# A graph layer and a mixture of experts on one core: up products of the ranked lists as seven block products

## The chip, the cores and the metric

The kernel runs on one NeuronCore of a Trainium2 chip. The metric is the device time of one execution in microseconds (us); less is better. The program has five engines that matter here: TensorE (PE in the profile, its weight loads PEld), VectorE (DVE), ScalarE (ACT), GpSimd (POOL) and SyncE (SP), which issues most transfers. Each engine works through its own instructions in a fixed order.

## The reference

There are 3327 tokens of 256 features. A graph attention layer over a 3327 x 3327 adjacency comes first, then a mixture of 16 experts of which each token uses its two best:

```python
x = x + _L0_gnn_ref(_layernorm(x), adj, W, a, gamma, beta)
...
xn = _layernorm(x)                                  # 256 features
logits = xn @ gate_w + gate_b                       # 16 experts
top_probs, top_idx = jax.lax.top_k(softmax(logits), 2)
top_probs = top_probs / sum(top_probs)
h1 = xn @ w1[e]                                     # 256 -> 512
h2 = xn @ w2[e]                                     # 256 -> 512
expert_out = (silu(h1) * h2) @ w3[e]                # 512 -> 256
x = x + sum over the two experts of top_probs * expert_out
```

All products of the experts are in float32. The two matrices w1 and w2 make the "up" products, w3 the "down" product.

## The kernel before

The graph part works first, in seven groups of up to four tiles of 128 tokens. As groups are finished, their tokens are gated, their normalised rows are stored to a buffer in HBM, and tables are made that say which token belongs to which expert. The experts' part then works through 19 lists of tokens (`take_list`, L1031). Lists 0 to 2 and 3 to 5 hold the tokens of experts 0 to 2, from the early and the late groups; lists 6 to 18 are the other 13 experts, ranked by the number of their tokens and called ranked lists here. A list has a fixed width, `ROOM` (L87): for lists 6 to 18 it is 512, 512, 480, 472, 416, 408, 400, 400, 392, 392, 376, 376 and 336 columns. Tokens beyond the room would be done in a loop behind (L1216), which these inputs do not enter.

One list goes as follows. GpSimd gathers the list's rows from HBM (`gather`, L960, one indirect DMA for each tile of 128 rows, into one of three buffers `XE`). VectorE works out the weights of the rows (`weigh`, L964). The rows are transposed to `xt`, with features on partitions: for lists below 8 on TensorE through the two PSUM banks "pt" (L1060, copied out by ScalarE at L1071), from list 8 on in `by_halves` (L1004) by DMA transposes of 16-bit halves, with copies in front (L1025 on ScalarE, L1026 on VectorE) and behind (L1028 on ScalarE, L1029 on VectorE). The copies behind write `xt`, of which there are two.

Then come the up products (`up_products`, L974). The 256 input features are KC = 2 blocks of 128, the 512 hidden features JC = 4 blocks of 128. For each hidden block j and each of w1 and w2, two matmuls of 128 x 128 weights against all n columns of the list add up over the input blocks in one of four PSUM banks "pa" (L976). Each program matmul is two instructions in the profile, since the operands are float32. ScalarE makes the gate `s` by Silu out of one bank (L1081), VectorE multiplies it with the other bank into `hid` (L1084). So a list has 16 program matmuls of n columns for its up products.

The down products (`down_products`, L978) take 128 tokens at a time: four matmuls with `hid` as weights and w3 of 256 columns as the moving side, in one of two banks "ph" (L987); for a last tile of up to 64 tokens, column tiles of the array share the work (L983). VectorE scales the rows by their token weights (L1102, and L1104 for the parts of a short tile); for lists 0 to 2 ScalarE does it for full tiles (L1100, `helped`). GpSimd adds the rows to the output by an indirect DMA with addition (`add_rows`, L989).

The order of all of this is not written out by hand. Every piece of work is registered with `plan.add`, with an engine, an estimated duration, a rank, the works that it follows and the buffers that it uses (`Plan`, L114). The planner places at each step the work that can start earliest, the lower rank first among equals (L171). A buffer kind has a number of slots (`SLOTS`, L372), and a further user waits for the oldest slot's users to end. Between engines it reckons 0.2 us (`HOP`). It draws 80 orders, replays them with disturbed durations and keeps the best (L203). The order then stands in the program; on the chip an engine waits at each instruction for what it needs. For a list i the rank on TensorE is (4, i, 0) for the transposes, (4, i, 1 + j) for the up products and (4, i, 9 + t) for the down products.

The weights of an expert are loaded by SP (`load_weights`, L325) into one of four sets of tiles, `w1e`, `w2e` and `w3e` (L332); the loads of list i are released by the gathers of list i - 2 (L1201).

Of the kernel before, what the change touches and what calls it, by code (L numbers as in the profile page):

```python
# [47 lines left out]
F32 = mybir.dt.float32  # L48
# [6 lines left out]
P = 128  # L55
# [3 lines left out]
D = 256  # L59
# [21 lines left out]
TURNED = 2 * EARLY + 2  # L81

# [134 lines left out]
def gnn_moe(ctx: ExitStack, tc: tile.TileContext, x, adj_t, W, a, gamma, beta, gate_w, gate_b, w1, w2, w3, out):  # L217
# [114 lines left out]
    def weight_tiles():  # L332
        return [POOLS["wmore"].tile([P, k, n], F32, name=name)
                for name, k, n in (("w1e", KC, HID), ("w2e", KC, HID), ("w3e", JC, D))]
# [33 lines left out]
    def few_h(key):  # L368
# [5 lines left out]
             "turned": 2}  # L374
# [19 lines left out]
        "turned": lambda key: POOLS["turns"].tile([P, 2 * KC, CAP], U16, name="turned_rows"),  # L394
        "y": lambda key: POOLS["gates"].tile([P, D], F32, name="y", bufs=SLOTS["y"]),
# [15 lines left out]
    def psum(key):  # L411
        return T[key]
# [565 lines left out]
    def down_products(py, w3e, hid, t, m):  # L978
        if PARTS[m] > 1:

            for j in range(JC):
                c = j % PARTS[m] * (P // PARTS[m])
                nc.tensor.matmul(py[c:c + m, :D], hid[:, j, t * P:t * P + m], w3e[:, j, :], start=(j < PARTS[m]),  # L983
                                 stop=(j >= JC - PARTS[m]), tile_position=(0, c))
            return
        for j in range(JC):
            nc.tensor.matmul(py[:m, :D], hid[:, j, t * P:t * P + m], w3e[:, j, :], start=(j == 0), stop=(j == JC - 1))  # L987
# [43 lines left out]
    def take_list(i, indexed, stored, weights, opened, order):  # L1031
# [14 lines left out]
        def w_of(k):  # L1046
            return WE[weights][k]
# [26 lines left out]
        for j in range(JC):  # L1074
# [3 lines left out]
                for b, key in enumerate(keys)]  # L1078

# [9 lines left out]
        for t, mm in tiles:  # L1089
            key, yk = ("ph", "list", i, t), ("y", i, t)  # L1090
            w = plan.add(PE, 8 * 0.217 / PARTS[mm] + 0.1 * (PARTS[mm] > 1), rank + (9 + t,), hids, lambda t=t, mm=mm, key=key: down_products(
                psum(key), w_of(2), hid(), t, mm), [key, hk] + ([wk] if weights else []))


            helped = i < EARLY and PARTS[mm] == 1
# [79 lines left out]
    def switch_pools():  # L1175
        gnn.close()
        POOLS["wmore"] = ffn.enter_context(tc.tile_pool(name="wmore", bufs=4))
        POOLS["hidden"] = ffn.enter_context(tc.tile_pool(name="hidden", bufs=2))
        POOLS["turns"] = ffn.enter_context(tc.tile_pool(name="turns", bufs=2))
        POOLS["gates"] = ffn.enter_context(tc.tile_pool(name="gates", bufs=3))  # L1180
# [24 lines left out]
    order, told = [], []  # L1205
# [82 lines left out]
```

## Time and profile before

| | us |
|---|---|
| median of 3 runs | 524.83 |
| lowest and highest run | 521.37, 528.43 |
| profiled execution, its time | 525.92 |
| profiled execution, its span | 524.0 |
| first up product of list 6, from the span's start | 285.06 |
| first down product of list 18, from the span's start | 512.63 |
| DVE, ACT, POOL busy over the span | 287.9, 173.1, 216.3 |

The span runs from the first to the last instruction in the trace; the execution's time has 1.9 us more around it. A line of the trace's timeline names the start and the length in us, the engine, the line of the kernel, the operation, output and inputs, the shape (partitions x elements), and how many instructions were merged; in brackets stand the idle time of the engine ahead of it and what ended that. A line of the waits names who waited for whom, the us in total, the times and the longest. PE's lengths overlap, since matmuls are pipelined; PEld is the load of weights, which runs beside the matmuls. TensorE ran at its full clock nearly throughout (a mean of 0.995).

### The profile page before, as it was taken

Reading aid. Unit: us, or ns where it says so; the run is one execution under the profiler, and the core shown is the slowest. Engines: PE = TensorE matmul, PEld = TensorE weight load, DVE = VectorE, ACT = ScalarE, POOL = GpSimd, SP = SyncE. Lnnn points to the kernel's source line nnn. Section 1 sums busy time; section 2 is a strip of 40 time slices with the busy share of each in tenths; the row PEclk is TensorE's granted clock in tenths of the full one; section 3 lists DMA queues with packets and bytes.
Section 4 is the critical chain, followed back from the end, with each engine's and each line's share of the span. In section 5 each row is a group of like instructions: output and inputs, shape, how many; then the busy total and the mean of one; then the engine's idle time right before and its main releaser. Section 6 shows DMA issues by size and latency. Waiting matters only on the chain. (4 is left out here: it accounts for less than half of the span.)

```text
span 524.0 us, 8563 instructions
## 1 busy us (share of the span) xinstructions
PE 508.0 (97%) x2923; PEld 400.0 (76%) x2924; DVE 287.9 (55%) x870; ACT 173.1 (33%) x464; POOL 216.3 (41%) x240
## 2 busy tenths in 40 slices
PE   9999999999999999999999979999999999999995
PEld 6789999999999999876778454665766566666773
DVE  5878564886969799768932234233333544334221
ACT  2462153635372741474222134132222212121110
POOL 4230022121031411737676667665644644224333
PEclk9999999999999999999999989999999999999999
DMA  8932889797879896454479778857867875542222
GB/s 274 357 134 79 306 254 306 244 321 248 264 218 366 284 350 205 147 184 115 83 236 346 145 167 171 179 122 191 155 130 186 200 180 99 130 138 30 29 31 28
DMA packets 85698, 100.01 MB, mean 191 GB/s; under 512 B 27150, under 2 KB 59154, under 8 KB 85652
## 3 DMA queue, kind: packets, MB, share of 16 engines
q1 hardware_dynamic: 74612, 85.42, 52.7%
q0 software_dynamic: 10768, 13.75, 15.9%
q8 instruction: 24, 0.39, 0.3%
q10 hardware_dynamic: 272, 0.26, 0.1%
q14 instruction: 22, 0.18, 0.1%
HBM read 81.55 MB, written 13.75 MB: 182 GB/s over the span
## 5 line engine op out<-in xcount | busy, mean ns | idle before, releaser
L589 PE MATMUL pa<-hi,mk 128*128 128x258 f32 x676 | 167.6, 289 | 0.0
L590 PE MATMUL pa<-lo,mk 128*128 128x256 f32 x676 | 163.2, 281 | 0.0
L990 POOL DMA_INDIRECT out<-y,out_index x61 | 96.4, 1580 | 110.0 <-DVE y L1102 92.7
L589 PEld LDWEIGHTS pa<-hi,mk 128*128 128x128 f32 x676 | 127.7, 189 | 1.1 <-issue 1.0
L590 PEld LDWEIGHTS pa<-lo,mk 128*128 128x128 f32 x676 | 127.5, 189 | 0.1
L976 PE MATMUL pa<-xt,w2e 128*128 128x512 f32 (+12 forms) x272 | 97.7, 482 | 0.0
L976 PE MATMUL pa<-xt,w1e 128*128 128x512 f32 (+12 forms) x272 | 97.1, 479 | 0.0
L987 PE MATMUL ph<-w3e,hid 128*128 128x256 f32 (+5 forms) x400 | 91.3, 384 | 4.2 <-DVE hid L1084 3.4
L987 PEld LDWEIGHTS ph<-w3e,hid 128*128 128x128 f32 (+5 forms) x400 | 75.2, 190 | 19.2 <-DVE hid L1084 3.8
L1081 ACT ACTIVATE s<-pa 128x512 f32<-128x512 f32 (+14 forms) x76 | 35.2, 464 | 135.9 <-PE pa L976 131.9
L976 PEld LDWEIGHTS pa<-xt,w1e 128*128 128x128 f32 x272 | 49.7, 190 | 35.8 <-issue 19.1
L976 PEld LDWEIGHTS pa<-xt,w2e 128*128 128x128 f32 x272 | 49.1, 190 | 36.2 <-issue 19.5
L961 POOL DMA_INDIRECT x<-normed,index x61 | 64.8, 1063 | 24.9 <-issue 19.2
L1084 DVE TENSOR_TENSOR hid<-s,pa 128x512 f32<-128x512 f32 (+14 forms) x76 | 39.3, 520 | 62.6 <-PE pa L976 53.3
L566 DVE TENSOR_SCALAR mk<-sg 128x2048 fp32r<-128x2048 f32 (+2 forms) x49 | 54.2, 1105 | 29.4 <-PE pa L590 28.3
L1102 DVE TENSOR_SCALAR y<-ph,weight 128x256 f32<-128x256 f32 (+10 forms) x54 | 25.9, 482 | 70.5 <-PE ph L987 63.3
L655 POOL TENSOR_TENSOR hp<-csum,c 128x512 f32<-128x512 f32 (+1 forms) x14 | 15.1, 1097 | 65.0 <-DVE c L651 65.0
L483 PE MATMUL ph<-w_sb,xnt 128*128 128x260 f32 x104 | 27.9, 405 | 1.0 <-DVE lo L489 1.0
L1025 ACT COPY halves<-x 128x1024 uint16<-128x1024 uint16 (+1 forms) x11 | 10.9, 987 | 52.5 <-DMA turned_rows<-halves 33.6
L483 PEld LDWEIGHTS ph<-w_sb,xnt 128*128 128x128 f32 x104 | 18.3, 195 | 5.2 <-DVE lo L489 1.4
L426 POOL TENSOR_SCALAR rs_x<-spread_x 128x4 f32<-128x4 f32 (+1 forms) x7 | 1.7, 241 | 48.3 <-ACT pay L432 45.2
L669 ACT ACTIVATE agg<-agg,c 128x64 f32<-128x64 f32 x76 | 18.8, 335 | 1.9 <-DVE c L651 1.8
(185 smaller groups left out, 485.2 us busy)
## 6 DMA issues: line engine op xcount, KB each, us to landing
sg<-in_adj_t SPq DMA_DIRECT2D x25, 1024.0 KB
sg<-in_adj_t SPq DMA_DIRECT2D x20, 768.0 KB
w1e<-in_ffn_w SPq DMA_DIRECT2D x15, 512.0 KB
w2e<-in_ffn_w SPq DMA_DIRECT2D x15, 512.0 KB
w3e<-in_ffn_w SPq DMA_DIRECT2D x15, 512.0 KB
normed<-pay SPq DMA_DIRECT2D x5, 520.0 KB
out<-x SPq DMA_DIRECT2D x5, 512.0 KB
sg<-in_adj_t SPq DMA_DIRECT2D x4, 576.0 KB
```

What stands on the lines that cost most here:

```text
L483: nc.tensor.matmul(ph[:, :H + D], T["xnt", g, t][:, k, :], w_sb[:, k, :], start=(k == 0), stop=(k == KC - 1))
L566: nc.vector.tensor_scalar(T[mk][:, :m, :n * P], T[sk][:, :m, :n * P], 0.0, None, op0=ALU.is_gt)
L589: nc.tensor.matmul(pa[:, :D + 2], lhs, HI[mg][:, i, H:], start=first, stop=False)
L590: nc.tensor.matmul(pa[:, :D], lhs, LO[mg][:, i, H:], start=False, stop=left[g, t] == 0)
L669: nc.scalar.mul(at, at, some("c")[:, 0, t, h:h + 1])
L961: nc.gpsimd.indirect_dma_start(out=xe[:, t, :], out_offset=None, in_=normed[:limit], in_offset=at_rows(idx, t), bounds_check=limit - 1, oo ...
L976: nc.tensor.matmul(p[:, :n], wt[:, k, j * P:(j + 1) * P], xt[:, k, :n], start=(k == 0), stop=(k == KC - 1))
L987: nc.tensor.matmul(py[:m, :D], hid[:, j, t * P:t * P + m], w3e[:, j, :], start=(j == 0), stop=(j == JC - 1))
L990: i = nc.gpsimd.indirect_dma_start(out=out, out_offset=at_rows(idx, t, m), in_=y[:m], in_offset=None, bounds_check=NP - 1, oob_is_err=Fals ...
L1081: nc.scalar.activation(T["gate", i, j][:, :n], psum(key)[:, :n], AF.Silu)
L1084: nc.vector.tensor_mul(hid()[:, j, :n], T["gate", i, j][:, :n], psum(key)[:, :n])
L1102: nc.vector.tensor_scalar(T[yk][:mm], psum(key)[:mm, :D], weight, None, op0=ALU.mult)
```

## The change

For lists 6 to 18 (`SEVEN` = 6) the up products are regrouped. Take a pair of hidden blocks (2 jp, 2 jp + 1), the two input blocks and the two halves of the list's columns. With weights a(c, k), c the hidden block of the pair and k the input block, and x blocks b(k, t), t the half of the columns, the four results are c(c, t) = a(c, 0) b(0, t) + a(c, 1) b(1, t), eight block products. Strassen's scheme (in Winograd's form) makes them with seven, out of sums of blocks:

- VectorE makes four sums of weight blocks for each list (one instruction each, 512 elements, for w1 and w2 and both pairs at once) and four sums of x blocks (half a list's width). Two of them overwrite a block in place; the others lie in slots of the older tiles "hp" and "agg" and in a new tile `xsum`.
- Each block product has one program matmul for w1 and one for w2, side by side in one bank (256 columns each).
- The products of a pair are p1, p5, p6, p2, p7, p3, p4 in this order. p1, p6 and p7 add up in one bank of "pt" (xx). ScalarE copies p1 from there to bank yy, where p2 is added; it copies p5 to SBUF (`qs`); after p6 VectorE writes the sum of xx and `qs` to bank zz, where p3 is added; after p7 ScalarE copies xx to bank vv, where p4 is added, and VectorE adds xx and `qs` to `c22`. So yy, zz, vv and `c22` are the four results.
- The four banks of "pa" become fixed banks for this (pq, py, pz, pv, one slot each). `fix_banks` opens them once by a bf16 matmul of 512 columns each, behind the last up products of list 5.
- Gates (ScalarE) and multiplies (VectorE) work on halves of the columns, eight of each for a list in place of four.
- The down products of these lists get the rank (4, i + 1, 9, t), that is behind the products of the next list, and a full tile's four matmuls are planned in two parts of two. The scaling of full tiles' rows goes to ScalarE.
- w1e and w2e become one tile.

The core of the diff:

```diff
-        return [POOLS["wmore"].tile([P, k, n], F32, name=name)
...
+        up = POOLS["wmore"].tile([P, 2, KC, HID], F32, name="w12e")
...
+             "turned": 2, "pq": 1, "py": 1, "pz": 1, "pv": 1, "qs": 2, "xsum": 2, "c22": 2}
...
+    FIXED = {}
+    CHAIN = []
+    def fix_banks():
+        for r in range(4):
+            FIXED[r] = psum(("pa", "fixed", r))
+            nc.tensor.matmul(FIXED[r], ones, ones[:, None, :].to_broadcast([P, CAP // P, P]), start=True, stop=True)
+    def by_sevenths(i, n, xts, loaded, fixed, xtk, wk, hk, weights):
+        half = n // 2
+        xsk, wsk, ask = ("xsum", i), ("hp", "list", i), ("agg", "list", i)
...
+        def combine(dst, one, other, op):
+            nc.vector.tensor_tensor(dst(), one(), other(), op=op)
+        def sums(cost, rank, after, uses, terms):
+            done, got = {}, []
+            for k, (name, dst, one, other, op, needs) in enumerate(terms):
+                done[name] = plan.add(DVE, cost, rank, after + [done[x] for x in needs],
+                                      lambda dst=dst, one=one, other=other, op=op: combine(dst, one, other, op), uses)
+            return done
+        S = sums(0.62, (2, i, 7), loaded, [wk, wsk, ask], [
+            ("1", lambda: ws(0), lambda: a(1, 0), lambda: a(1, 1), ALU.add, ""),
+            ("2", lambda: ws(1), lambda: ws(0), lambda: a(0, 0), ALU.subtract, "1"),
+            ("3", lambda: a(1, 0), lambda: a(0, 0), lambda: a(1, 0), ALU.subtract, "1"),
+            ("4", lambda: ws(2), lambda: a(0, 1), lambda: ws(1), ALU.subtract, "2")])
+        X_ = sums(0.1 + 0.55e-3 * n, (2, i, 6), xts, [xtk, xsk, ask], [
+            ("1", lambda: xs(0), lambda: b(0, 1), lambda: b(0, 0), ALU.subtract, ""),
+            ("2", lambda: xs(1), lambda: b(1, 1), lambda: xs(0), ALU.subtract, "1"),
+            ("3", lambda: b(0, 1), lambda: b(1, 1), lambda: b(0, 1), ALU.subtract, "1"),
+            ("4", lambda: xs(2), lambda: b(1, 0), lambda: xs(1), ALU.subtract, "2")])
+        base = xts + loaded
+        hids = []
+        def pair(jp):
+            xx, qq, yy, zz, vv, qs, cc = [(name, "seven", i, jp) for name in ("pt", "pq", "py", "pz", "pv", "qs", "c22")]
+            def product(number, after, key, lhs, rhs, first, more=()):
+                def emit(key=key, lhs=lhs, rhs=rhs, first=first, jp=jp):
+                    for w in range(2):
+                        nc.tensor.matmul(psum(key)[:, w * (CAP // 2):w * (CAP // 2) + half], lhs()[:, w, jp], rhs(),
+                                         start=first and w == 0, stop=True, skip_group_check=True)
+                return plan.add(PE, 4 * (0.44 * half / CAP + 0.003), (4, i, jp, number), after, emit, [key, xtk, xsk, wk, wsk, ask] + list(more))
+            def copy(src, key, at):
+                return plan.add(ACT, 0.14 + 0.9e-3 * n, (1, i, jp), [at], lambda: nc.scalar.copy(
+                    T[key][:, :, :half] if key == qs else both(psum(key)), both(psum(src))), [src, key])
+            def added(after, dst, more):
+                return plan.add(DVE, 0.16 + 1.02e-3 * n, (1, i, jp), after, lambda: nc.vector.tensor_tensor(
+                    dst(), both(psum(xx)), T[qs][:, :, :half], op=ALU.add), [xx, qs] + more)
+            p1 = product(0, base, xx, lambda: a(0, 0), lambda: b(0, 0), True)
+            p5 = product(1, [S["1"], X_["1"], p1, fixed], qq, lambda: ws(0), lambda: xs(0), True)
+            cy = copy(xx, yy, p1)
+            cq = copy(qq, qs, p5)
+            p6 = product(2, [cy, S["2"], X_["2"]], xx, lambda: ws(1), lambda: xs(1), False)
+            p2 = product(3, [cy], yy, lambda: a(0, 1), lambda: b(1, 0), False)
+            az = added([cq, p6], lambda zz=zz: both(psum(zz)), [zz])
+            p7 = product(4, [az, S["3"], X_["3"]], xx, lambda: a(1, 0), lambda: b(0, 1), False)
+            p3 = product(5, [az, S["4"]], zz, lambda: ws(2), lambda: b(1, 1), False)
+            cv = copy(xx, vv, p7)
+            ac = added([p7, cv, cq], lambda cc=cc: T[cc][:, :, :half], [cc])
+            p4 = product(6, [cv, X_["4"]], vv, lambda: a(1, 1), lambda: xs(2), False)
+            for j, t, made, key in ((0, 0, p2, yy), (0, 1, p3, zz), (1, 0, p4, vv), (1, 1, ac, cc)):
+                gk = ("gate", i, 2 * jp + j)
+                def part(w, key=key):
+                    return T[key][:, w, :half] if key[0] == "c22" else psum(key)[:, w * (CAP // 2):w * (CAP // 2) + half]
+                def gate(gk=gk, t=t, part=part):
+                    nc.scalar.activation(T[gk][:, t * half:(t + 1) * half], part(0), AF.Silu)
+                def multiply(gk=gk, j=j, t=t, jp=jp, part=part):
+                    nc.vector.tensor_mul(T[hk][:, 2 * jp + j, t * half:(t + 1) * half], T[gk][:, t * half:(t + 1) * half], part(1))
+                s = plan.add(ACT, 0.14 + 0.9e-3 * half, (1, i, jp, 9), [made], gate, [key, gk])
+                hids.append(plan.add(DVE, 0.16 + 1.02e-3 * half, (2, i), [s], multiply, [key, gk, hk]))
+        for jp in range(JC // 2):
+            pair(jp)
+        return hids
...
+        if i >= SEVEN:
+            if i == SEVEN:
+                CHAIN.append(plan.add(PE, 0.9, (4, i, -1), UPS, fix_banks, [("pa", "fixed", r) for r in range(4)]))
+            hids = by_sevenths(i, n, xts, opened, CHAIN[0], xtk, wk, hk, weights)
+        for j in range(JC if i < SEVEN else 0):
             keys = [("pa", "list", i, j, b) for b in range(2)]
             ups = [plan.add(PE, 4 * max(0.44 * n / CAP, 0.12), rank + (1 + j,), xts + opened, lambda j=j, b=b, key=key: up_products(
                 psum(key), w_of(b), xt(), j, n), [key, xtk] + ([wk] if weights else []))
                 for b, key in enumerate(keys)]
+            UPS.extend(ups)
             def gate(j=j, key=keys[0]):
                 nc.scalar.activation(T["gate", i, j][:, :n], psum(key)[:, :n], AF.Silu)
@@ -1088,11 +1205,16 @@
         ends = []
         for t, mm in tiles:
             key, yk = ("ph", "list", i, t), ("y", i, t)
-            w = plan.add(PE, 8 * 0.217 / PARTS[mm] + 0.1 * (PARTS[mm] > 1), rank + (9 + t,), hids, lambda t=t, mm=mm, key=key: down_products(
-                psum(key), w_of(2), hid(), t, mm), [key, hk] + ([wk] if weights else []))
-
-
-            helped = i < EARLY and PARTS[mm] == 1
+            parts = (0, 1) if i >= SEVEN and PARTS[mm] == 1 else (None,)
+            w = None
+            for part in parts:
+                w = plan.add(PE, (8 * 0.217 / PARTS[mm] + 0.1 * (PARTS[mm] > 1)) / len(parts),
+                             (4, i + 1, 9, t) if i >= SEVEN else rank + (9 + t,), hids + [w],
+                             lambda t=t, mm=mm, key=key, part=part: down_products(psum(key), w_of(2), hid(), t, mm, part),
+                             [key, hk] + ([wk] if weights else []))
+            helped = (i < EARLY or i >= SEVEN) and PARTS[mm] == 1
```

## The prediction

> **What bounds the kernel now.** I read the page's busy times first, then the busy time of each engine in the stretch of the ranked lists (lists 6 to 18, the only ones that the change touches), then TensorE's timeline there, then who waits for whom.
>
> Busy time of the whole span, and of the stretch from the first product of list 6 to the last down product:
>
> ```profile
> PE 508.0 (97%) x2923; PEld 400.0 (76%) x2924; DVE 287.9 (55%) x870; ACT 173.1 (33%) x464; POOL 216.3 (41%) x240
> ...
> core 0: us, PE busy (x) PEld busy (x) DVE busy (x) ACT busy (x) POOL busy (x), PEclk, DMA share, GB/s
> 285.06:517.97 232.91, 228.70 (x817) 145.28 (x815) 81.17 (x165) 52.08 (x76) 118.81 (x90) 0.99 0.63 134
> ```
>
> TensorE is busy 228.7 of 232.9 us; VectorE 81 and ScalarE 52. Matmul durations overlap, so the cost of a group is the distance of starts. TensorE's timeline (start, length, x instructions), at 512, 128 and 400 columns, and one list's down products:
>
> ```profile
> 286.78 1.88 PE L976 MATMUL pa<-xt,w2e 128*128 128x512 f32 x4
> 288.50 1.88 PE L976 MATMUL pa<-xt,w1e 128*128 128x512 f32 x4
> ...
> 276.06 0.61 PE L976 MATMUL pa<-xt,w1e 128*128 128x128 f32 x4
> 276.51 0.61 PE L976 MATMUL pa<-xt,w2e 128*128 128x128 f32 x4
> ...
> 402.14 5.34 PE L987 MATMUL ph<-w3e,hid 128*128 128x256 f32 x24
> 407.42 0.63 PE L983 MATMUL ph<-w3e,hid 128*24 128x256 f32 x8
> ...
> 413.46 1.51 PE L976 MATMUL pa<-xt,w2e 128*128 128x400 f32 x4
> 414.80 1.51 PE L976 MATMUL pa<-xt,w1e 128*128 128x400 f32 x4
> ```
>
> Each program matmul is two instructions, so a group of four is one up product over both halves of K: 1.72 us at 512 columns, 1.34 at 400 (1.26 at 376 and 1.13 at 336 in the same view). These lie on 3.346 ns a column + 0.004 us. At 128 and at 112 columns it is 0.45: a floor near 0.11 us an instruction. Down products cost 0.216 an instruction (32 in the 6.91 us from 347.82 to 354.73).
>
> Who waits, TensorE in lists 6 to 18, and the one place where it does:
>
> ```profile
> PE ph L987 <- DVE hid L1084: 3.4, 1, 3.4
> PE ph L987 <- DVE y L1102: 0.8, 1, 0.8
> ...
> 302.18 1.05 ACT L1025 COPY halves<-x 128x1024 uint16<-128x1024 uint16 x1 [7.71 <-DMA x<-normed,index]
> 303.75 0.69 DVE L1084 TENSOR_TENSOR hid<-s,pa 128x512 f32<-128x512 f32 x1 [0.52 <-ACT s L1081]
> 304.50 7.27 PE L987 MATMUL ph<-w3e,hid 128*128 128x256 f32 x26 [3.37 <-DVE hid L1084]
> ```
>
> TensorE's issue order is fixed and it almost never waits. The exception is instructive: ScalarE stood 7.7 us in front of a copy whose gathered rows were late, a gate behind it came late, then the product, then TensorE.
>
> **The change part by part.** *Products.* A list's 8 up groups become 14 block products of four instructions at half the columns. Before: 8 x (0.003346 n + 0.004). After: 14 x (0.001673 n + 0.004). Saved: 0.003346 n - 0.024 us a list; the widths of the 13 lists sum to 5472, so 18.3 - 0.3 = **18.0 us**. The narrowest block is 168 columns, 0.57 us by the line, above the floor of 0.45.
>
> A weight load's own row gives 190 ns (49.7 us over 272 in the page's groups), yet four loads and their matmuls pass in 0.45 us at 128 columns: loads overlap, and I take the line. The Trainium skill speaks against that ("Perfetto Trace Analysis", Identifying the Most-Contended Engine): TensorE's headroom is to be judged by the load slices' summed time, not by matmul busy time. Loads rise from 32 to 56 a list, 56 x 0.19 = 10.6 us against 9.45 of products at 400 columns; if they bound the nine lists of 416 columns and less, 9 x 10.64 - 82.4 = 13 us of the 18 would go and the sum below would end at 527.
>
> *Opening the four fixed banks* (four bf16 matmuls of 512 columns). No row has their pace: the warm-up's bf16 rows of that width last 0.63 us, 2.5 in all at most; instructions of the lists pass in 0.43, 1.7 in all; the neighbour products of the graph part, 256 or 258 columns, start 0.12 apart (214.72, 214.84, 214.96 in TensorE's timeline), about 0.24 for 512. I take these last, 1.0, as the operands nearest in kind to a single pass; the ends are 0 (TensorE finds an idle place) and 2.5. At 283 us TensorE has work, so it counts.
>
> *The chain inside a pair.* Before, up products wait for nothing but inputs and a free bank. Now p6 waits for the copy of p1, p7 for the sum after p6, p4 for the copy of p7. At 400 columns: a product 0.675; ScalarE starts 0.20 after TensorE passes to its next group (a gate at 413.66, the next group at 413.46); copy 0.50 (gate rows of 400 columns 0.502, PSUM copies of 384 0.486); VectorE starts 0.27 after (a multiply at 415.07, the next group at 414.80), sum 0.57 (its row of 400 columns); TensorE starts 0.06 after a release (303.75 + 0.69 against 304.50). So p1 0 to 0.68, p5 to 1.35, copy 0.88 to 1.38, p6 at 1.44 (gap 0.09) to 2.12, p2 to 2.79, sum 2.39 to 2.96, p7 at 3.02 (gap 0.23) to 3.70, p3 to 4.37, copy 3.90 to 4.40, p4 at 4.46 (gap 0.09). 0.41 us a pair if nothing else ran; by the same steps 0.16 at 512 columns (product 0.86, copy 0.59, sum 0.69), 0.2 at 480 and 472, 0.5 at 336: 9.0 us for the 26 pairs. No row shows a copy from PSUM to PSUM. Its nearest are these PSUM reads; at 0.37 (the 257-column row) the two 0.09 gaps are gone, at 0.60 (512-column gate) a pair loses 0.61.
>
> What hides it: the second pair's p1 (its bank of two is free) and the previous list's down products, which the new rank puts behind this list's products and cuts in halves of 4 x 0.216 = 0.86: six pieces and a short one a list, against six gaps of 0.09 to 0.23. A piece covers any of them. Without it the 9.0 us stand. The present lists lose 0.2 beyond their sum (16.68 from one list's start to the next at 400 columns, against 10.74 + 5.18 + 0.56); I add 0.15 for each of lists 8 to 18: 1.7.
>
> List 6 has one short list before it to fill with, and list 7's PE transposes use the two banks that now hold the chain's accumulator, so that list 7 can start only behind their two ScalarE copies (0.59 each). I charge four uncovered pairs, 0.6, and the copies, 1.2: 1.8, bounds 0 and, if list 6's x sums (four of 0.42) come late too, 3.5.
>
> *VectorE*, a list of 400: weight sums 4 x 0.69 (rows of 256, 768 and 1024 columns: 0.419, 0.952, 1.216), x sums 4 x 0.36, PSUM sums 4 x 0.57, products of halves 8 x 0.36 (rows 0.286 at 128 and 0.431 at 272), row copies 0.8 + 0.75, list weights 0.4, the short tile's 2.0: 13.3 us of TensorE's 15.2 (14 x 0.675 + 24 x 0.216 + 0.56). Full, but under, and durations overlap by some 0.08. The three scalings of full tiles move to ScalarE, which then has 6 x 0.50 + 8 x 0.33 + 3 x 0.47 + 1.0 + 1.35 = 9.4. Both keep time to spare, and I cost their work at nothing by TensorE's cover; if that fails the rivals price it. The new sums read two SBUF operands; such sums beside GpSimd:
>
> ```profile
> L661 DVE TENSOR_TENSOR agg<-agg,c x7: 414/419/1261, 204.9 to 226.8; 128x256 f32<-128x256 f32 x7
> ...
> 219.55 0.43 DVE L661 TENSOR_TENSOR agg<-agg,c 128x256 f32<-128x256 f32 x1
> ...
> 219.31 1.00 POOL L961 DMA_INDIRECT x<-normed,index  x1 [0.31 <-issue]
> ```
>
> Beside a GpSimd sum it took up to 1.26 us, beside a gather's descriptors 0.43: the lists have only the latter, so nothing is added.
>
> *Late rows.* The wait at 302 us cost 3.4 of the present time. ScalarE's next gates were held 3 us at 292 too, with no loss, since four banks of up products were ahead. Now a held ScalarE stops the chain at the next copy. I add 2.4 (all 5.8 us that VectorE, too, waited at 302, less the 3.4 already paid); from -3.4, if the new order misses that wait, to +5.8.
>
> *Queues.* Weights and transposes stay on SP, gathers and output rows on POOL; a sum that waits for weights holds VectorE, but loads leave early: list 13's at 374.18, its first product at 417.49.
>
> *Tail.* After the last product a half gate and product (0.32 + 0.35) replace 0.45 + 0.50; the first tile's early half-sums cover them: +0.2.
>
> Sum: -18.0 + 1.0 + 1.7 + 1.8 + 2.4 + 0.2 = **-10.9**. The profiled execution took 525.92 us (524.0 span, 1.9 around it): 515.0. It stands 1.1 above the median of 524.83, so against the median 513.9. I forecast **514**.
>
> **The rivals.** *Gaps uncovered.* The planner's filling doesn't hold on the chip, and pairs lose their gaps: 9.0 in place of the 1.7 and of 0.6 in the start: 514 + 6.7 = 521. For it: TensorE's order is fixed, and a filler placed after a wait covers nothing. Against: the present lists lose 0.2.
>
> *VectorE holds the chain (slower).* On a queue that is 88% full (13.3 of 15.2), the sum after p6 stands behind a weight sum (0.69) in each pair, and the gates' multiplies that free the banks behind the other pair's sum (0.57): 1.26 us a pair, 26 x 1.26 = 33 in place of those 2.3, 514 + 30.5 = 544. Break-even lies at (10.9 + 2.3) / 26 = 0.51 a pair, 2% slower at 0.91. For it: VectorE's 81 us grow to some 13 x 12.7 = 165 of 222. Against: a filler is longer than either obstacle.
>
> *Nothing lost.* Fillers cover all, the wait at 302 goes: -18.0 + 1.0 - 3.4 + 0.2 = -20.2: 504.6.
>
> **How the numbers follow.** The forecast's case 0.52, its own range 508 to 519 (late rows and start at their bounds); gaps uncovered 0.24 (517 to 529); VectorE holding the chain 0.15 (529 to 560); nothing lost 0.09 (503 to 508). The range 507 to 534 leaves out most of the last and two thirds of the third. 2%, about what a measurement of this kernel tells from no change, is 514.3 below and 535.3 above. Faster: 0.38 of the first case and 0.09: 0.47. Slower: 0.12 of the third. Same: the rest, 0.41.
>
> **What would show it.** Up products of 400 columns should pass in 0.67 us each, fourteen a list; if 0.76, four loads of 0.19, loads bind. A list of 400 should take some 15.3 us from start to start, 16.7 before. Waits of TensorE for ScalarE copies and VectorE sums, summed over lists 8 to 18, should be under 3 us; near 10 is the first rival, over 20 the second, and VectorE would then be seen busy just before the late sum. A hold of ScalarE at a late gather should appear as TensorE's longest wait. The forecast is wrong if the planner's new order also moves the graph part, before 215 us, which I hold unchanged.

## The result: no gain, and the profile after

The changed kernel takes 527.25 us (median of 20 runs, 525.12 to 532.76); the kernel before took 522.63 us beside it (20 runs, 518.94 to 528.43). The ratio is 1.01, its 95% interval 1.0069 to 1.013: about 1% slower, where 2% faster was forecast. Some runs of a kernel fall into a slower state, over 1.5% above its fastest run; medians and ratios in this document are those of the other runs. The profiled execution of the changed kernel took 529.58 us, with a span of 527.4.

Busy times, from the page of the changed kernel:

```profile
PE 497.3 (94%) x3239; PEld 449.5 (85%) x3240; DVE 349.0 (66%) x1035; ACT 235.2 (45%) x637; POOL 222.1 (42%) x240
```

TensorE works 10.7 us less than before (508.0), yet the span is 3.4 longer. So it stands idle more. I cut both spans at the first up product of list 6 and at the start of the last scaling of rows, and do so for every kernel below:

| us, profiled execution | before | changed |
|---|---|---|
| start to the first product of list 6 | 285.06 | 285.88 |
| from there to the last scaling (the lists) | 232.95 | 229.97 |
| from there to the end of the span (the tail) | 5.99 | 11.55 |
| span | 524.0 | 527.4 |

The lists became 3.0 us shorter, not 18; the tail grew by 5.6. In the changed kernel's numbering the products of seven are L1046, the copies from bank to bank L1052, the sums out of PSUM L1056, gates L1078, multiplies L1081, down products L1099 and (short tile) L1095, the scalings on ScalarE L1222, the additions to the output L1102, the copies of gathered rows L1137 (ScalarE) and L1138 (VectorE).

*The products are as fast as forecast.* TensorE's timeline of the changed kernel, at 400 columns:

```profile
404.01 0.84 PE L1046 MATMUL pa<-xt,w12e 128*128 128x200 f32 x4
404.69 0.84 PE L1046 MATMUL pt<-xt,w12e 128*128 128x200 f32 x4
405.37 0.84 PE L1046 MATMUL pa<-agg,hp 128*128 128x200 f32 x4
```

Starts are 0.68 apart; 0.675 was forecast. Late lists run as planned: p1 of lists 15 to 18 start at 453.06, 468.27, 483.11 and 497.31, that is 15.21, 14.84 and 14.20 us a list, 0.16 to 0.24 above the sums of their products (14.98, 14.60, 14.04). The loss lies earlier.

*Who waits.* From the waits of the changed kernel, lists 6 to the end (us in total, times, longest), first TensorE's, then the longest of ScalarE that a DMA ends:

```profile
PE ph L1099 <- ACT y L1222: 7.0, 3, 3.4
PE ph L1095 <- ACT y L1222: 2.8, 2, 1.8
PE pt L1046 <- DVE pa L1056: 2.2, 2, 1.9
PE pa L1046 <- ACT pa L1052: 1.6, 1, 1.6
...
ACT halves L1137 <- DMA x<-normed,index: 20.6, 8, 3.8
```

With 0.2 for the transposes TensorE waits 13.8 us where it waited 4.2. The largest part, 9.8, is for ScalarE's scaling of output rows, which frees the banks of the down products. One such place in the timeline of the changed kernel:

```profile
337.51 1.05 ACT L1137 COPY halves<-x 128x1024 uint16<-128x1024 uint16 x1 [2.89 <-DMA x<-normed,index]
...
338.46 0.36 ACT L1078 ACTIVATE s<-pa 128x240 f32<-128x240 f32 x1
...
339.17 0.46 ACT L1222 ACTIVATE y<-ph,weight 128x256 f32<-128x256 f32 x1
...
339.67 3.82 PE L1099 MATMUL ph<-w3e,hid 128*128 128x256 f32 x16 [1.42 <-ACT y L1222]
...
339.90 1.90 POOL L1102 DMA_INDIRECT out<-y,out_index  x1 [7.11 <-ACT s L1078]
```

ScalarE stood 2.89 us before a copy whose gathered rows had not landed. Behind it in ScalarE's order were gates and then the scaling; until the scaling is done, TensorE has no bank for the next down product. The same happens at 358, 378, 416 and 433 us, where TensorE waits 2.23, 3.39, 1.01 and 1.76 us.

Why the rows are late can be followed from one list to the next in the same timeline (`weight<-hit`, L978, is the end of working out a list's row weights; L970 are gathers):

```profile
343.53 0.47 ACT L1222 ACTIVATE y<-ph,weight 128x256 f32<-128x256 f32 x1 [1.35 <-PE ph L1099]
...
344.78 0.16 DVE L978 TENSOR_REDUCE weight<-hit 128x4 f32<-128x8 f32 x1
...
348.15 1.08 POOL L970 DMA_INDIRECT x<-normed,index  x1 [0.30 <-issue]
...
358.17 1.04 ACT L1137 COPY halves<-x 128x1024 uint16<-128x1024 uint16 x1 [3.69 <-DMA x<-normed,index]
...
359.82 0.46 ACT L1222 ACTIVATE y<-ph,weight 128x256 f32<-128x256 f32 x1
...
360.33 3.79 PE L1099 MATMUL ph<-w3e,hid 128*128 128x256 f32 x16 [2.23 <-ACT y L1222]
...
387.44 0.16 DVE L978 TENSOR_REDUCE weight<-hit 128x4 f32<-128x8 f32 x1 [3.03 <-ACT y L1222]
```

The last scaling of list 7 ends at 344.00; only then are the weights of list 11 made, and the buffer of its rows is free for list 14. The gathers of list 14 go out behind GpSimd's additions from 348.15 on, ScalarE waits for them, and the next scaling and TensorE wait in turn. At 387.44 the view names the link itself: the weights of list 13 waited 3.03 us for the last scaling of list 9.

*A second loss follows some of these waits.* Windows of the changed kernel (busy time of PE, PEld, DVE, ACT and POOL, then the granted clock):

```profile
285.88:515.90 230.02, 216.20 (x1126) 193.94 (x1124) 136.94 (x319) 113.73 (x249) 119.84 (x87) 0.98 0.63 133
...
381.50:387.00 5.50, 5.50 (x18) 4.15 (x19) 2.88 (x8) 1.24 (x4) 4.67 (x3) 0.69 0.72 105
436.00:441.00 5.00, 5.00 (x25) 4.84 (x20) 3.08 (x7) 0.95 (x2) 4.39 (x3) 0.66 0.67 155
293.00:298.00 5.00, 4.75 (x14) 3.88 (x15) 1.79 (x5) 2.18 (x5) 3.73 (x4) 0.66 0.90 120
```

In three stretches of 5 us the mean clock was 0.66 to 0.69: some 1.7 us lost in each. The kernel before had one (behind its wait at 302).

*The tail.* GpSimd's additions of the last list in the changed kernel:

```profile
511.55 1.62 POOL L1102 DMA_INDIRECT out<-y,out_index  x1 [0.30 <-issue]
...
518.92 1.57 POOL L1102 DMA_INDIRECT out<-y,out_index  x1 [5.75 <-issue]
```

List 17's down products are done behind list 18's products, so the last of its additions leaves at 511.55. The first addition of list 18 leaves 5.75 us behind the end of that one, though its rows were scaled at 512.39. The program orders the additions of different lists (they may add to the same row), while those of one list follow each other after 0.30. Before, the same addition left at 515.45, right behind its scaling at 514.56.

### The profile page after: what moved, and what is told of

Read it like the earlier page. It is cut to its first block, busy times and chain, and to the rows that moved or that the text cites. A ratio compares the mean times of both kernels' runs of the same rounds, so it can differ in the third digit from the quotient of the medians.

```text
span 527.4 us, 9541 instructions
## 1 busy us (share of the span) xinstructions
PE 497.3 (94%) x3239; PEld 449.5 (85%) x3240; DVE 349.0 (66%) x1035; ACT 235.2 (45%) x637; POOL 222.1 (42%) x240
## 5 line engine op out<-in xcount | busy, mean ns | idle before, releaser
L1102 POOL DMA_INDIRECT out<-y,out_index x61 | 101.3, 1661 | 106.2 <-ACT y L1222 68.8
L1099 PE MATMUL ph<-w3e,hid 128*128 128x256 f32 (+5 forms) x400 | 97.2, 386 | 7.1 <-ACT y L1222 7.0
L1099 PEld LDWEIGHTS ph<-w3e,hid 128*128 128x128 f32 (+5 forms) x400 | 74.3, 190 | 18.6 <-ACT y L1222 9.0
L970 POOL DMA_INDIRECT x<-normed,index x61 | 65.8, 1078 | 27.7 <-issue 18.0
L1046 PE MATMUL pt<-xt,w12e 128*128 128x256 f32 (+8 forms) x208 | 47.4, 353 | 2.2 <-DVE pa L1056 2.2
L1078 ACT ACTIVATE s<-pa 128x256 f32<-128x256 f32 (+8 forms) x78 | 26.8, 345 | 43.6 <-PE pa L1046 41.4
L1046 PEld LDWEIGHTS pt<-xt,w12e 128*128 128x128 f32 x208 | 37.4, 194 | 7.0 <-DVE pa L1056 2.9
L1081 DVE TENSOR_TENSOR hid<-s,pa 128x256 f32<-128x256 f32 (+8 forms) x78 | 28.8, 371 | 14.7 <-ACT s L1078 13.6
L1222 ACT ACTIVATE y<-ph,weight 128x256 f32<-128x256 f32 (+4 forms) x50 | 23.1, 470 | 33.0 <-PE ph L1099 31.7
L1052 ACT COPY pa<-pt 128x512 f32<-128x512 f32 (+8 forms) x52 | 25.1, 498 | 17.8 <-PE pt L1046 15.3
L1056 DVE TENSOR_TENSOR c<-pt,qs 128x512 f32<-128x512 f32 (+8 forms) x26 | 15.5, 596 | 25.5 <-ACT pa L1052 25.5
L985 PE MATMUL pa<-xt,w12e 128*128 128x352 f32 (+3 forms) x128 | 26.8, 360 | 0.0
L1046 PE MATMUL pa<-xsum,w12e 128*128 128x256 f32 (+8 forms) x104 | 22.9, 343 | 1.6 <-ACT pa L1052 1.6
L1138 DVE COPY halves<-x 128x1024 uint16<-128x1024 uint16 (+1 forms) x11 | 7.8, 708 | 25.1 <-DMA x<-normed,index 24.8
L1056 DVE TENSOR_TENSOR pa<-pt,qs 128x512 f32<-128x512 f32 (+8 forms) x26 | 15.7, 602 | 12.7 <-PE pt L1046 12.1
```

Of the source, the lines that this page charges most:

```text
L970: nc.gpsimd.indirect_dma_start(out=xe[:, t, :], out_offset=None, in_=normed[:limit], in_offset=at_rows(idx, t), bounds_check=limit - 1, oo ...
L985: nc.tensor.matmul(p[:, :n], wt[:, k, j * P:(j + 1) * P], xt[:, k, :n], start=(k == 0), stop=(k == KC - 1))
L1046: nc.tensor.matmul(psum(key)[:, w * (CAP // 2):w * (CAP // 2) + half], lhs()[:, w, jp], rhs(), start=first and w == 0, stop=True, skip_gro ...
L1056: return plan.add(DVE, 0.16 + 1.02e-3 * n, (1, i, jp), after, lambda: nc.vector.tensor_tensor(dst(), both(psum(xx)), T[qs][:, :, :half], o ...
L1078: nc.scalar.activation(T[gk][:, t * half:(t + 1) * half], part(0), AF.Silu)
L1081: nc.vector.tensor_mul(T[hk][:, 2 * jp + j, t * half:(t + 1) * half], T[gk][:, t * half:(t + 1) * half], part(1))
```

## The experiments

My theory after the result, called *deferral*: the seven products are sound, and the new rank of the down products, (4, i + 1, 9, t) in place of (4, i, 9, t), costs the time. It does the down products of a list behind the next list's products, so the scalings and additions come a list later. Later additions make the tail. A later scaling frees a set of row weights later (four sets: list 11's weights need list 7's scaling), which frees a buffer of gathered rows later, and on GpSimd gathers stand behind additions; so rows land late, the copies of rows stop ScalarE and VectorE, and TensorE stops. Each run below was measured beside the kernel before, which took 523.85, 525.74 or 525.07 us there, so the ratios compare better than the times. Every edit lets the planner make a new order, also of the work ahead of the lists. The rivals: *full engines* (VectorE and ScalarE have too much to do), the planner's *guess of a gather's landing* (2.6 us) alone, and the prediction's own claim that the deferred down products are needed as cover.

**The rank alone put back**, all else of the change kept; run twice:

```diff
-                             (4, i + 1, 9, t) if i >= SEVEN else rank + (9 + t,), hids + [w],
+                             rank + (9 + t,) if i >= SEVEN else rank + (9 + t,), hids + [w],
```

> All down products at their own list's rank, as before the change: nothing is deferred, and the chain of the pairs has only the other pair and parts of down products as cover. Theory 'deferral': the wait at the end (5.75 us) and most of the waits for scalings (9.8) go, uncovered gaps of up to 9 us come: 517 to 524. Rival 'gaps uncovered' (from the prediction, that fillers are what keeps TensorE busy): the gaps cost more than what comes back, over 527. Rival 'full engines': the same time, 526 to 529.

> The change with the down products at their own list's rank, once more and in more rounds, for a firm interval. If the first measurement holds: 508 to 511, ratio 0.970 to 0.980.

Measured: 509.25 us, ratio 0.9724 (0.9664 to 0.9784); in more rounds 509.54, ratio 0.9719 (0.9662 to 0.9775). This is faster than both kernels, by 2.8% than the one before, and better than the 517 to 524 that I had expected of *deferral*: the gaps that I had added did not come. In the first trace the lists take 215.84 us and the tail 5.95: 14.1 and 5.6 less than in the changed kernel, which with 0.1 at the start is all of the 19.8 between the spans. (In the second trace the lists take 218.65, because TensorE waits 3.84 us once, at 303 us.) TensorE's waits in the first:

```profile
PE pt L1046 <- DVE pa L1056: 2.3, 1, 2.3
PE ph L1099 <- DVE hid L1081: 0.8, 1, 0.8
PE ph L1099 <- ACT y L1222: 0.6, 1, 0.6
```

With 0.2 for transposes 3.9 us, 9.9 less; and one slow-clock stretch in place of three, 3.4 less: 13.3 of the 14.1. List 14's gathers leave at 340.12 to 344.20 (348.15 to 352.17 in the changed kernel, 341.92 to 346.25 before). What covers the handoffs of the chain then is seen in TensorE's timeline:

```profile
359.11 0.96 PE L1046 MATMUL pa<-xt,agg 128*128 128x236 f32 x4
359.90 0.87 PE L1046 MATMUL pa<-agg,hp 128*128 128x208 f32 x4
360.61 0.96 PE L1046 MATMUL pa<-xsum,w12e 128*128 128x236 f32 x4
```

A product of 236 columns (list 9) is followed by one of 208 (list 10) and again by one of 236: pairs of neighbouring lists interleave, and the down products run as one block of 32 instructions behind them (at 364.22). They are not needed as cover. The claim falls.

**The rank alone in the old kernel**: before, with only the rank of lists 6 to 18 changed; no products of seven.

```diff
-            w = plan.add(PE, 8 * 0.217 / PARTS[mm] + 0.1 * (PARTS[mm] > 1), rank + (9 + t,), hids, lambda t=t, mm=mm, key=key: down_products(
+            w = plan.add(PE, 8 * 0.217 / PARTS[mm] + 0.1 * (PARTS[mm] > 1), (4, i + 1, 9, t) if i >= 6 else rank + (9 + t,), hids, lambda t=t, mm=mm, key=key: down_products(
```

> The kernel before with one part of the change alone: the down products of lists 6 to 18 get the rank behind the next list's products; no block products of seven. The deferral theory: the deferral alone costs, in the old kernel too: the last list's additions wait for those of list 17 to land (the tail from TensorE's end to the span's end grows from 6.1 to about 11, +5), and the weight slots and gather buffers come free later, so that some rows are late; 527 to 536 where before is 522.6, ratio 1.01 to 1.025. If only the block products make the rank harmful (their chain stops where a copy is late), it is the tail alone or less: 522 to 527.

Measured: 530.79 us, ratio 1.0111 (1.005 to 1.0172). In its trace the lists take 234.37 us (+1.4) and the tail 10.98 (+5.0). Its additions at the end, then its waits for rows:

```profile
521.15 1.57 POOL L990 DMA_INDIRECT out<-y,out_index  x1 [4.96 <-issue]
```

```profile
PE ph L987 <- DVE hid L1084: 4.3, 1, 4.3
...
ACT halves L1025 <- DMA x<-normed,index: 28.8, 7, 8.5
```

The kernel before, in the same view:

```profile
ACT halves L1025 <- DMA turned_rows<-halves: 33.6, 5, 7.5
ACT halves L1025 <- DMA x<-normed,index: 18.9, 5, 7.7
```

So the rank costs 5.7 us by itself (530.79 - 525.07 beside it), nearly all in the tail. It makes rows late in the old kernel too: ScalarE waits 28.8 us for rows in place of 18.9, VectorE 22.8 in place of 9.3 (its copies, L1026). (The 33.6 us that ScalarE waited for transposes before are 0.6 here: the rows now come last.) But there it costs TensorE only 1.2 us of further waits: old up products need nothing from ScalarE but a bank. In the changed kernel, with rows late as well, the new rank costs the lists 14.1. So that loss comes of the new rank together with another part of the change, not of the rank alone. Which part is not shown: of TensorE's waits there, 9.8 us are for the scalings, which the change also moved to ScalarE, and 3.8 for copies and sums of the chain; the new rank with the scalings left on VectorE was not run.

**Two more sets of row weights** (the changed kernel otherwise):

```diff
-             "few": 3, "few_h": 3, "xe": 3, "hid": 2, "gate": 3, "y": 6, "w": 4, "weight": 4, "halves": 2,
+             "few": 3, "few_h": 3, "xe": 3, "hid": 2, "gate": 3, "y": 6, "w": 4, "weight": 6, "halves": 2,
```

> Six buffers for the lists' row weights in place of four, nothing else. Theory 'deferral': the down products, now ranked behind the next list's products, are scaled late; a list's weigh step waits for the weight buffer of the list four back, so for those late scalings; the buffer of gathered rows is then freed late, the gathers are issued late, and the copies of rows on ScalarE and VectorE stand in front of the scalings and gates. With six buffers that link is cut: TensorE's waits for ScalarE's scalings (9.8 us in lists 6 to 18 of the changed kernel) fall below 4, the time falls by 5 to 12, to 515 to 522. The end of the run (GpSimd idle 5.75 us ahead of the last list's first addition) stays. Rival 'full engines': TensorE waits because VectorE and ScalarE have too much to do; then nothing moves, 526 to 528. Rival 'landing guess': rows are simply planned to land too early; then under 3 us are gained.

Measured: 519.85 us, ratio 0.9934 (0.9898 to 0.997). No wait of TensorE for a scaling is left; ScalarE waits for rows 5.2 us in place of 20.6, and the lists take 214.18. The tail stays (11.59):

```profile
509.59 1.57 POOL L1102 DMA_INDIRECT out<-y,out_index  x1 [5.76 <-issue]
```

List 6 starts at 292.33, 6.5 later: the planner's order before the lists changed too, and this takes back part of the gain. Yet list 14's gathers leave at 332.61 to 336.55, 15.5 us earlier than in the changed kernel. With the lines at 343 and 387 us above, this shows the sets of row weights as the link between a late scaling and late rows.

**The tail alone**: lists 17 and 18 at their own rank, the others deferred.

```diff
-                             (4, i + 1, 9, t) if i >= SEVEN else rank + (9 + t,), hids + [w],
+                             (4, i + 1, 9, t) if SEVEN <= i < NL - 2 else rank + (9 + t,), hids + [w],
```

> Only the last two lists keep their down products at their own rank, so list 17's come before list 18's products again. Theory 'deferral': the additions of list 17 are issued some 6 us earlier, the wait of 5.75 us on GpSimd ahead of list 18's first addition is gone or under 1.5 us, while list 18's chain loses its fillers (at most 2 x 0.5 us): 4 to 5 us less, 522 to 523.5. Rival 'full engines': the end is not set by the additions, so no change or the lost fillers, 527 to 528.

Measured: 522.39 us, ratio 0.9989 (0.9938 to 1.0041), 0.011 under the changed kernel's ratio. The tail is 5.87 again, the lists still take 231.31. The two losses are separate. The time is in the range expected of *deferral*; by the ratio the gain is some 6 us, a little more than the 4 to 5 expected.

**A longer guess of the gathers' landing**, in the changed kernel and in the old one:

```diff
-                         landing=2.6) for t, _ in tiles]
+                         landing=5.0) for t, _ in tiles]
```

> The planner is told that gathered rows land 5.0 us after their issue in place of 2.6; no engine gets other work, only the order may move. Rival 'landing guess': the copies of rows move behind scalings and gates that are ready, TensorE's waits for scalings fall from 9.8 to below 3 us, 515 to 519. Theory 'deferral': the rows are late by their issue as well, but a copy that is not in front of others does no harm: 4 to 10 us less, 517 to 523, waits at the end unchanged. Rival 'full engines': 526 to 528.

> The kernel before the change with the planner's landing time of gathered rows at 5.0 in place of 2.6. It tells whether that guess costs the old kernel as well: theory 'deferral' says that there rows are gathered some 10 us ahead of their copies, so only the one wait at 302 us (3.4) can go: 519 to 524, no more than 1% below before. Rival 'landing guess' (the guess is at fault by itself, whatever the rank): 512 to 518.

Measured: changed kernel 515.81 us, ratio 0.9869 (0.9804 to 0.9935); old kernel 527.8, ratio 1.0051 (1.0011 to 1.0092), a miss. The changed kernel's time is the one that *landing guess* forecast (515 to 519), a little below the 517 to 523 of *deferral*. With the later guess the planner sets the copies of rows later: no wait of TensorE for a scaling is left, and the lists take 211.78 us. The tail is still 11.37, as *deferral* had it. In the old kernel the lists too got shorter (229.63 against 232.95), but list 6 starts at 292.32 in place of 285.06, so the time before the lists took back more than was won. That start also moves in the changed kernel (289.35). So the guess matters for the lists, and these two runs cannot tell its worth alone, since the order ahead of the lists changes with it. Nor is the guess by itself the fault: with the rank put back and the guess left at 2.6 the time is lower (509.25, the intervals of the ratios do not overlap), and the tail is mended too. A late scaling makes the rows late; a guess that is too short puts their copies where they stop others. In these traces, mending either one cures the lists.

**Rank and guess together**:

> Seven products with the down products at their own rank (as in the run that gave a ratio of 0.972) and the landing time at 5.0 as well. The two cuts meet the same link: theory 'deferral' says that with the rank mended little is left to gain, one wait of 2.3 us and its slower clock near 293 us at the most: 505 to 510. If the landing guess were a cause of its own, another 8 to 12 us would go, below 503.

Measured: 512.51 us, ratio 0.9798 (0.9726 to 0.9869), above the 505 to 510 expected, and no better than the rank alone. Its lists take 211.85 us, 4 less, and list 6 starts at 289.59, 3.8 later: what the lists gain is lost ahead of list 6. No further 8 to 12 us went, so the guess is no cause of its own.

**Rank and six sets of row weights**:

> Down products at their own rank, and six weight slots in place of four. The deferral theory: at the own rank the y of list i is made early enough, so two more slots give nothing: 507 to 512, within 0.5% of the same kernel with four. If the slots hold up the rows even then: 503 to 506.

Measured: 509.49 us, ratio 0.9725 (0.967 to 0.9781), against 0.9719 for the rank alone in the same comparison: nothing, as deferral says. At its own rank a scaling is early enough for four sets.

**Full engines: the changed kernel without the eight SBUF sums.** It leaves out the four sums of weights and four of x of each list; the products take plain blocks, so it does not compute the reference.

```diff
+            return b(r % 2, 1)
...
+            return a(1, r % 2)
...
-                done[name] = plan.add(DVE, cost, rank, after + [done[x] for x in needs],
-                                      lambda dst=dst, one=one, other=other, op=op: combine(dst, one, other, op), uses)
+                done[name] = None
```

> The changed kernel without the eight sums of weight and x blocks (the products take plain blocks in their place), so this leaves out 8 VectorE instructions a list, some 4 us of 13, and the output is not the reference's. Theory 'deferral': VectorE's load is not what delays the rows; the waits for scalings and the wait before the last additions stay, 522 to 527. Rival 'full engines': with VectorE a third emptier the waits of TensorE (13.8 us) fall below 5 and the time to 513 to 518.

Measured: 529.13 us, ratio 1.0071 (1.0031 to 1.0112). Its window of the lists:

```profile
285.00:515.00 230.00, 216.33 (x1133) 194.07 (x1131) 95.09 (x227) 115.56 (x251) 115.86 (x87) 0.98 0.64 136
```

VectorE is busy 95.1 us in place of 137.8 in the same stretch of the changed kernel, and the ratio is the changed kernel's within its interval (1.0069 to 1.013). (The time lies above both ranges expected; by the ratio it is 526 us beside the 522.63 of the first comparison, which is in the range of *deferral*.) In the one trace the lists take 225.93 us, 4.0 less, with rows still late: ScalarE waits 11.9 us for them in place of 20.6, TensorE 4.1 for scalings in place of 9.8, and 10.8 in all in place of 13.8. So a third of VectorE's work gone makes the waits shorter in the trace, but the runs do not show it in the time; *full engines* falls as the main cause.

**The scalings of full tiles back on VectorE**, at the own rank:

```diff
-            helped = (i < EARLY or i >= SEVEN) and PARTS[mm] == 1
+            helped = i < EARLY and PARTS[mm] == 1
```

> Down products at their own rank, and the scalings of full tiles of the ranked lists back on VectorE. If moving them to ScalarE was right (VectorE full at 13.3 of 15.2 us a list, and 3 x 0.5 more on it): sums and multiplies come later, 511 to 516. If it is neutral, since either engine has time and TensorE has other work: 508 to 511. If ScalarE was the engine that held up the banks: 505 to 508.

Measured: 512.53 us, ratio 0.98 (0.9743 to 0.9857), against 0.9719 (0.9662 to 0.9775) beside it. The medians lie 3.0 us apart, in favour of ScalarE; the intervals overlap, and one trace of each (spans of 509.3 and 510.5) doesn't show a cause. I leave it at that.

One thing follows from these runs together. With the down products at their own rank and the pairs interleaved, four different orders of the planner took 509.3 to 512.5 us; the five versions with the new rank, for all lists or all but two, took 515.8 to 529.1. So the gain is not the luck of one order.

**No interleaving of pairs**: at the own rank, p1 of each pair must follow p4 of the pair before, so that only down products can fill the gaps.

```diff
-            p1 = product(0, base, xx, lambda: a(0, 0), lambda: b(0, 0), True)
+            p1 = product(0, base + LAST[-1:], xx, lambda: a(0, 0), lambda: b(0, 0), True)
...
+            LAST.append(p4)
```

> Seven products with the down products at their own rank, and each pair's first product made to follow the last product of the pair before it, so that pairs no longer run side by side. It prices the uncovered chain, which the prediction put at 9.0 us for the 26 pairs (0.16 each at 512 columns, 0.41 at 400, 0.5 at 336). If that working holds and it is the other pair that covers the gaps: 509 + 9 = 516 to 520. If down products cover them alone: 508 to 511. If a handoff costs more than the rows said: over 525.

Measured: 543.11 us, ratio 1.0371 (1.03 to 1.0443), above the 516 to 520 of my own working; it is the third case that I had named (a handoff costs more than the rows said). The lists take 244.26 us, 28.4 more than with interleaving (first trace): 1.1 a pair, where the prediction priced bare gaps at 9.0 for all. A pair of 392 columns in which no copy or sum is held up, in its timeline:

```profile
473.19 0.83 PE L1047 MATMUL pt<-xt,w12e 128*128 128x196 f32 x4
...
473.85 0.83 PE L1047 MATMUL pa<-agg,hp 128*128 128x196 f32 x4
...
474.57 0.93 PE L1047 MATMUL pt<-agg,hp 128*128 128x196 f32 x4
...
475.34 0.83 PE L1047 MATMUL pa<-xt,w12e 128*128 128x196 f32 x4
...
476.22 0.93 PE L1047 MATMUL pt<-xt,w12e 128*128 128x196 f32 x4
...
476.99 0.83 PE L1047 MATMUL pa<-xt,agg 128*128 128x196 f32 x4
...
477.71 0.93 PE L1047 MATMUL pa<-xsum,w12e 128*128 128x196 f32 x4
```

The next pair starts at 478.48. Seven products take 5.29 us, and 7 x 0.66 is 4.62: 0.67 lost, where 0.41 was priced (at 400 columns). The gaps themselves are as priced: the products just ahead of p6, p7 and p4 pass in 0.72, 0.88 and 0.72 in place of 0.66, so gaps of 0.06, 0.22 and 0.06 us, 0.34 in all. The rest, 0.33, is that a product which starts on a signal (p6, p7, p4) passes in 0.77, not 0.66. So handoffs that nothing covers cost about 26 x 0.67 = 17 us. The other 11 of the 28.4 I put down to sums queued behind other work on VectorE (one, at 470.30, started behind a short tile's scalings and TensorE waited 1.22 us). The waits fit this, 12.5 us in 9 places for such sums against 2.3 in one place with interleaving, but I did not test it by itself:

```profile
PE pt L1047 <- DVE pa L1057: 12.5, 9, 2.8
```

## Why the prediction was wrong, point by point

The forecast was 514, from -10.9 against the profiled 525.92; it took 529.58 there, +3.7.

- *Products, -18.0*: right. 0.68 us each at 400 columns; with the rank put back the lists lose 17.1 us in the first trace and 14.3 in the second, so 18.0 less 0.9 or 3.7 for everything else that the change adds there. The Trainium skill ("Perfetto Trace Analysis", Identifying the Most-Contended Engine) judges TensorE's headroom by the busy share of its load slices, beside the arithmetic done. My estimate from that, 0.76 a product if loads bound, did not come true: starts are 0.68 apart.
- *Opening the banks, +1.0*: right, 0.86 (four from 281.52 to 282.38).
- *The chain, 1.7, and the start, 1.8*: right in sign, smaller than priced where rows are in time (0.9 or 3.7 for these two and the late rows together, with the rank put back; 5.9 was priced). But its working was half wrong: the cover is the next pair, not the down products, and uncovered handoffs cost 0.67 a pair at 392 columns, not 0.41, since a start on a signal takes 0.11 more, which I had left out. The sign that I had named held: in lists 8 to 18 TensorE waited 0.3 us for copies and sums, under 3. It watched the chain, and the loss was elsewhere. A copy from PSUM to PSUM took 0.47 at 392 columns and 0.57 at 512, as priced.
- *VectorE and ScalarE at nothing*: nearly right for VectorE (without the sums 0 to 4 us are won); it was busy 137 of 230 us in the lists, less than the estimated 165 of 222. ScalarE has time as well (114 of 230 us), but the order of its work let scalings stand behind copies of late rows.
- *Late rows, +2.4, bounds -3.4 and +5.8*: this term failed. It measured 14.1 (lists of the changed kernel against those with the rank put back; 11.3 by the second trace). I had the mechanism, a copy of late rows in front of work that TensorE needs, from the wait at 302 us, and priced it as one event, with the chain's next copy as the victim. The new rank made it a habit, and the victim was mostly the scaling (9.8 us of TensorE's waits, against 1.6 for copies), which frees the banks of the down products.
- *The step that failed behind it*: "the previous list's down products, which the new rank puts behind this list's products". I booked this move as cover only. A moved step takes along all that it frees: the scaling, the additions on GpSimd, the set of weights, the buffer of rows, the gather that waits for it. "Weights and transposes stay on SP, gathers and output rows on POOL" counted the queues, not the order in them. The profile of before shows the raw material: copies that wait for rows in 5 of 11 lists.
- *Tail, +0.2*: failed for the same reason; it measured +5.6. I looked at what follows the last product, not at what now stands ahead of the last list's additions.
- *Rivals*: gaps uncovered (521) and VectorE holding the chain (544) are not what happened; TensorE's waits for VectorE's sums are 2.2 us. That 527 lies in the range that I gave to gaps uncovered (517 to 529) is chance. With the old rank the change takes 509.3 to 509.5, between nothing lost (504.6) and the forecast.

What stays open: whether queued sums are all of what the serial pairs lose beyond 0.67 each, whether the scalings on ScalarE or the chain made late rows so dear, whether the scalings belong on ScalarE, and the waits near 293 and 303 us, of which some stayed in every version that starts list 6 at 285 to 286 us.

## What to carry to other kernels

When a change moves a step, list everything that the step releases (buffers, slots, the transfers behind them) and the last use at the end of the kernel; price the move there before you book it as cover. If TensorE comes to wait for more work of ScalarE and VectorE, which go through theirs in a fixed order, older stalls there, harmless so far, can become stalls of TensorE: find them in the waits of before, and give the buffers or the order that remove them. If a change bundles a new scheme with a new order, measure each alone: here the change without the new rank is worth 2.8%, and the new rank alone costs 1.1%.

## What the runs showed of the hardware

- TensorE's clock fell behind some waits as short as 1.8 us: to a mean of 0.66 to 0.69 over some 5 us behind waits of 1.93 us (293.25), 3.39 (381.50) and 1.76 (435.60), but 1.00 behind 2.23 (360.33) and 1.42 (339.67). In windows of 1 us the first stretch has 0.50 from 294.20 to 296.20 and 1.00 again from 297.20. The Trainium skill ("TensorE: Matmul & The Clock Gate", Why this matters for your kernels) asks for no idle gap above about 3 us; here gaps of 1.8 us were already followed by the slow clock, and not every one.
- A group of four that starts on a signal passes in about 0.1 us more than one that follows without a stop (0.77 against 0.66 at 196 columns).
- An addition to HBM that must follow another one went out 5.0 to 5.8 us behind the end of that one's issue (4.96, 5.53, 5.75 and 5.76 at the end of four versions); gathered rows of list 14 could be copied 5.0 us behind the end of the last gather's issue (353.16 to 358.17).
